# Closing four finished batches, and turning the next ones, one at a time inside the steps of a gated graph network

## The chip, the cores and the metric

The kernel runs on one core of one Trainium2 chip. The time is the device time of the whole program in microseconds (us), the median of several executions. The kernel before takes 1812.43 us (1811.12 to 1814.71 in 4 runs beside the changed kernel). All runs told of here, of both kernels and of every experiment, are in the fast state. The clock that TensorE was granted, as a mean over a run, lay between 0.995 and 0.999 of full speed, except in the three kernels in which TensorE stops longest: `closing_only` (0.990 to 0.992), `pin_turn` (0.985 to 0.988) and `pin_order34` (0.982 to 0.985). The experiments ran in three later calls on other chips; the kernel before took 1813.1, 1812.22 and 1812.23 us there, so differences of 1 us between experiments of different calls say nothing. The spans in the profiles are about 2 us shorter than the times, so spans are compared with spans and times with times.

## The reference, cut to what matters

```python
def _L1_gnn_ref(input, in_matrix, out_matrix, w3_w, ..., time_step):     # both matrices are adj
    def step(h, _):
        m_in  = jnp.einsum('nm,bmd->bnd', in_matrix, h)
        m_out = jnp.einsum('nm,bmd->bnd', out_matrix, h)
        av = jnp.concatenate([m_in, m_out], axis=-1)
        u3 = h @ u3_w.T + u3_b
        z = sigmoid(av @ w3_w.T + w3_b + u3)
        r = sigmoid(av @ w4_w.T + w4_b + u3)
        hv = tanh(av @ w5_w.T + w5_b + (r * h @ u5_w.T + u5_b))
        h = (1.0 - z) * h + z * hv
    ...                                                     # 5 steps

x = _layernorm(x + _L0_gnn_ref(x, adj, ...), axis=-1)       # x: 16 batches of 1024 x 128
x = _layernorm(x + _L1_gnn_ref(x, adj, adj, ...), axis=-1)
```

All is float32. The kernel takes the 16 batches in four groups of four. A group goes through its five steps, and then it has to be *closed*: the last h is added to the saved x, and the sum is normalized and stored.

## The kernel before: the parts that matter

h lies in two layouts. `rows` has nodes on the partitions, for the products with adj; `hid` has features on the partitions, for the gates. Within a step a batch goes from `hid` to `rows` by a VectorE turn of 32x32 blocks and a trip over DRAM (`turn_rows`, `fetch_rows`). At a change of group two more turns are needed: the last h goes back to node rows for the closing, and the first h of the next group, which was loaded as rows, goes to `hid`.

```python
    y_of = [ypad[0], ypad[1], hvs.rearrange("p h x -> p (h x)"), ypad[0]]

    def finish_early(q, k):                    # closing, first half: by TensorE
        nc.sync.dma_start(y_of[k], saved_rows(q * QUAD + k))
        finish(q, k, y_of[k])                  # two times: 4 transposes, then a VectorE add out of PSUM

    def turn_hidden(k, stage):                 # turn of the next first h: 4 small VectorE turns a batch
        ...
        for q in range(NQ): for s in range(STEPS):          # cut
            ...
                else:                          # first step of the next group
                    outer_sums(rows)
                    before = [call(finish_early, q - 1, k) for k in range(QUAD)]
                    norm = [call(normalize, q - 1, k, y_of[k]) for k in range(QUAD)]
                    fetch = [call(fetch_hidden, k) for k in range(QUAD)]
                    hooks = {
                        12: {5: [before[1]], 2: [fetch[0], before[2]], "end": [fetch[1], before[3]]},
                        3: {1: [fetch[2]], 2: [fetch[3]]},
                        67: {6: [norm[1]], 7: [norm[2]], 4: [norm[3]]},
                        54: {"end": [call(drain, 99, 0)]},
                    }
```

The products with adj come in four chains, `12`, `3`, `67` and `54`; each has seven products (1 to 7) that go through three banks of PSUM and are taken out by a copy or an add:

```python
        after = {
            1: lambda: nc.scalar.copy(fb, fa),
            ...
            7: lambda: nc.vector.tensor_add(x22, fb, x22),    # frees bank pb for product 4
            3: lambda: nc.vector.tensor_add(x12, fc, x12),
            4: lambda: nc.scalar.copy(x21, fb),               # the gates of the step need this one
        }
```

A hook `{67: {1: f}}` is run while the program is written, ahead of product 1 of chain `67`. What is not pinned is put into an engine's queue by the planner that lays the program out, so the order in a queue is partly the planner's.

Of the kernel before, what the change touches and what calls it, by code (L numbers as in the profile page):

```python
# [15 lines left out]
STEPS = 5  # L16
# [4 lines left out]
def kernel(  # L21
# [63 lines left out]
    turned = [dram.tile([16, P, 64], F32, name=f"turned{i}") for i in range(3)]  # L85
    hidden = [dram.tile([16, P, 64], F32, name=f"hidden{i}") for i in range(QUAD)]
# [146 lines left out]
    def layernorm(y, tag, store, now=False):  # L233
# [4 lines left out]
        for c in range(n + 1):  # L238
            if c < n:
                pin(nc.vector.bn_stats(stats[:, c, :], y[:, c, :]))  # L240
            if c > 0:
                pin(nc.vector.bn_aggr(mv[:, c - 1, :], stats[:, c - 1, :]))
# [16 lines left out]
        if now == "DVE":  # L259
            for c in range(n):  # L260
                nc.vector.tensor_scalar(
                    y[:, c, :], y[:, c, :], mv[:, c, 0:1], rstd[:, c : c + 1],
                    ALU.subtract, ALU.mult,
                )
            put()
        elif now:
            for c in range(n):
                apply(c)
            put()
        else:  # L270
            for c in range(n):
                waiting.append((slot[0], lambda c=c: tc.keep_in_program_order(apply(c))))
            waiting.append((slot[0], put))

# [48 lines left out]
    def chain(tag, src, turned, ns, results, hooks, order=(1, 5, 6, 2, 7, 3, 4)):  # L323
# [32 lines left out]
        for a in order:  # L356
# [12 lines left out]
            with tc.high_priority():  # L369
                after[a]()  # L370
# [145 lines left out]
    def turn_rows(k, h=None):  # L516
        cols, n = half_of(h)
        t = ypad[k % 2][:, cols]
        op = nc.vector.transpose(
            t.rearrange("p (to n j c) -> p n to c j", to=4, n=n, c=2),  # L520
            hid[:, k, cols].rearrange("p (n to i c) -> p n to c i", to=4, n=n, c=2),
        )
        tc.keep_in_program_order(nc.sync.dma_start(
            between(k, h).rearrange("g p x -> p g x"), t.rearrange("p (g x) -> p g x", x=64)
        ))
        return op

    def fetch_rows(k, h=None):
        cols, n = half_of(h)
        src = between(k, h).rearrange("(to n) (s j) x -> to j (n s) x", n=n, s=4)  # L530
        for to in range(4):
            tc.keep_in_program_order(nc.sync.dma_start(
                rows[ts(to, SQ), k, cols].rearrange("j (m x) -> j m x", x=64), src[to]
            ))

    def turn_hidden(k, stage):

        v = rows[:, k].rearrange("p (n c a j) -> p n c a j", n=4, c=2, a=4)
        for f in range(2):
            t = stage(f)  # L540
            for a in range(2):
                nc.vector.transpose(
                    t[:, ts(a, QT)].rearrange("p (n i c) -> p n c i", n=4, c=2),
                    v[:, :, :, 2 * f + a],
                )
            nc.sync.dma_start(
                hidden[k][ts(f, 8)].rearrange("g p x -> p g x"),
# [10 lines left out]
    def to_hidden(k):  # L558
        turn_hidden(k, lambda f: agg[:, 2 * (k % 2) + f, HALF:])
        fetch_hidden(k)  # L560
# [93 lines left out]
    y_of = [ypad[0], ypad[1], hvs.rearrange("p h x -> p (h x)"), ypad[0]]  # L654

    def finish_early(q, k):
        nc.sync.dma_start(y_of[k], saved_rows(q * QUAD + k))
        finish(q, k, y_of[k])
# [42 lines left out]
    for q in range(NQ):  # L701
        for s in range(STEPS):
            tag = f"{q}_{s}"
            if s == 0:
# [11 lines left out]
                else:  # L716
                    outer_sums(rows)
                    before = [call(finish_early, q - 1, k) for k in range(QUAD)]
                    norm = [call(normalize, q - 1, k, y_of[k]) for k in range(QUAD)]
                    fetch = [call(fetch_hidden, k) for k in range(QUAD)]  # L720
                    hooks = {
                        12: {5: [before[1]], 2: [fetch[0], before[2]], "end": [fetch[1], before[3]]},
                        3: {1: [fetch[2]], 2: [fetch[3]]},
                        67: {6: [norm[1]], 7: [norm[2]], 4: [norm[3]]},
                        54: {"end": [call(drain, 99, 0)]},
                    }
            else:
                hooks = {54: {}}
            hooks[54][4] = [call(gate_half, tag, 0, 0)]
            aggregate(tag, rows, hooks, s > 0)  # L730
            last = s == STEPS - 1
            end = last and q == NQ - 1
# [8 lines left out]
            gates(tag, 1)  # L741
            update(tag, 0, not last)
            if not last:
                fetch_rows(0)
            gates(tag, 2)
            update(tag, 1, not last)
            if last:
                finish_early(q, 0)
                normalize(q, 0, y_of[0])
                for k in range(2):  # L750
                    turn_hidden(k, lambda f: first[:, k, ts(f, HALF)])
            else:
                fetch_rows(1)
            gates(tag, 3)
            if last:
                sums_of(rows, (1, 2))
                sums_of(rows, (3,))
                for k in range(2):
                    turn_hidden(2 + k, lambda f: first[:, k, ts(f, HALF)])
            update(tag, 2, not last)  # L760
            update(tag, 3, not last)
# [35 lines left out]
```

## Time and profile before

| | kernel before |
|---|---|
| median time | 1812.43 us |
| span in the profile | 1810.0 us |
| one inner step | 77.17 us |
| the last step of a group with the first of the next | 159.29, 159.00, 160.43 us |
| data moved by DMA | 140.37 MB, 78 GB/s |

The prediction below shows the busy table, the three changes and an inner step. Two views that it leaves out matter later. The first is an inner step that is longer than the others, in the table by stage (stretch, length, then busy time of TensorE, weight loads, VectorE, ScalarE and GpSimd with instruction counts, granted clock, DMA share, GB/s):

```profile
778.22:856.52 78.30, 77.41 (x278) 53.23 (x276) 52.87 (x76) 31.45 (x52) 0.00 (x0) 1.00 0.26 58
```

TensorE is idle here for 0.89 us: VectorE had waited 1.41 us for a fetch of `rows` (781.02), and its sum of line 289 came late. Nothing in the prediction counts this wait, and it is one that another layout can lose by chance. The second is the end of chain `54` on TensorE in an inner step (start, duration, instruction):

```profile
1135.83 1.03 PE L361 MATMUL pc<-e,tsum 128*128 128x256 f32 x4
1136.85 1.14 PE L361 MATMUL pb<-s,inner 128*128 128x256 f32 x4
1137.82 1.03 PE L361 MATMUL pb<-a,inner 128*128 128x256 f32 x4
1138.68 1.03 PE L361 MATMUL pc<-e,tsum 128*128 128x256 f32 x4
```

Product 3 (into pc) is split: four matmuls, then product 4 (into pb), then the other four. Four matmuls should start 0.86 us before the next group, as the last two rows do. Here the distances are 1.02 and 0.97, so the split costs 0.27 us, and it does so in every inner step of this kernel.

### The profile page before, as it was taken

The page shows a single profiled execution, that of the slowest core. Times are in us where ns is not written, and L with a number is a line of the kernel's source. Part 1 is how long each engine was busy: PE and PEld are TensorE (multiplying, and loading weights), DVE is VectorE, ACT ScalarE, POOL GpSimd, SP SyncE. Part 2 cuts the span into 40 slices and gives each one's busy share as a digit, 9 for nine tenths or more (in the row PEclk, how much of TensorE's full clock was granted, in tenths as well). Part 3 has the DMA queues.
Part 4 walks back from the last instruction along what each step waited for, and adds up shares of the span by engine and source line. Part 5 has one row for each costly group of instructions (what it writes and reads, how often), then busy time and mean ns, then how long its engine had stood idle before and what let it go on. Part 6 is the DMA issues. An engine that isn't in the chain of part 4 may idle for free.

```text
span 1810.0 us, 19922 instructions
## 1 busy us (share of the span) xinstructions
PE 1787.7 (99%) x6805; PEld 1269.2 (70%) x6805; DVE 1293.8 (71%) x2316; ACT 793.4 (44%) x1418; POOL 98.0 (5%) x142
## 2 busy tenths in 40 slices
PE   8999999999999999999999999999999999999998
PEld 7888884866758576675857757586675858667584
DVE  7987776676766958576676957667577775767667
ACT  2345555344342554434244463434434553443426
POOL 0112220000000010000000200000000100000004
PEclk9999999999999999999999999999999999999999
DMA  6233262140323334132142423214043331403222
GB/s 224 71 128 138 95 158 68 32 93 12 82 47 93 91 97 93 23 71 51 43 106 81 93 70 70 62 32 93 12 105 95 92 83 23 93 18 76 52 54 82
DMA packets 352564, 140.37 MB, mean 78 GB/s; under 512 B 338128, under 2 KB 339024, under 8 KB 352464
## 3 DMA queue, kind: packets, MB, share of 16 engines
q1 hardware_dynamic: 351600, 135.96, 29.5%
q10 hardware_dynamic: 864, 3.15, 0.4%
q8 instruction: 54, 0.88, 0.2%
q14 instruction: 46, 0.38, 0.1%
HBM read 80.35 MB, written 58.72 MB: 77 GB/s over the span
## 4 chain that ended last, share of the span: by engine, by line
PE 87%; DVE 7%; DMA 2%; ACT 1%; POOL 1%; issue 1%; SPq 0%; DVEq 0%; POOLq 0%
PE pb L361 23%; PE pa L361 13%; PE pc L361 12%; PE pu L462 7%; PE pu L451 7%; PE seeded L467 7%; PE ph L480 7%; PE ph L479 7%; PE pc_x L361 2%; PE pa_x L361 2%; PE seeded L428 1%; DMA rows<-saved 1%; POOL rstd L246 1%; PE pt L566 1%; DVE agg L411 1%
## 5 line engine op out<-in xcount | busy, mean ns | idle before, releaser
L361 PE MATMUL pb<-e,inner 128*128 128x256 f32 x864 | 206.7, 380 | 3.7 <-ACT pb L347 2.6
L466 DVE TENSOR_TENSOR tsum<-tsum,hid 128x512 f32<-128x512 f32 x160 | 107.1, 683 | 114.6 <-ACT tsum L465 114.2
L361 PEld LDWEIGHTS pb<-e,inner 128*128 128x128 f32 x864 | 167.1, 194 | 24.6 <-ACT pb L347 4.2
L490 ACT ACTIVATE tsum<-ph,bh 128x512 f32<-128x512 f32 x158 | 108.6, 687 | 145.0 <-PE ph L480 144.8
L462 PE MATMUL pu<-agg,w_t 128*128 128x512 f32 x320 | 166.0, 608 | 0.5 <-DVE agg L411 0.5
L480 PE MATMUL ph<-tsum,u_t 128*128 128x512 f32 x320 | 163.5, 592 | 0.1
L496 DVE TENSOR_TENSOR tsum<-tsum,hid 128x512 f32<-128x512 f32 x158 | 108.1, 684 | 77.6 <-ACT tsum L490 77.4
L479 PE MATMUL ph<-agg,w_t 128*128 128x512 f32 x320 | 163.5, 592 | 0.0
L467 PE MATMUL seeded<-agg,w_t 128*128 128x512 f32 x320 | 161.0, 592 | 0.0
L451 PE MATMUL pu<-hid,u_t 128*128 128x512 f32 x320 | 152.0, 594 | 2.0 <-DVE ypad L574 2.0
L361 PE MATMUL pb<-s,inner 128*128 128x256 f32 x576 | 151.3, 385 | 0.3 <-DVE agg L351 0.2
L361 PE MATMUL pb<-a,inner 128*128 128x256 f32 x576 | 144.6, 379 | 0.0
L465 ACT ACTIVATE tsum<-pu,br 128x512 f32<-128x512 f32 x160 | 110.2, 688 | 74.3 <-PE pu L462 69.9
L361 PE MATMUL pc<-e,inner 128*128 128x256 f32 x560 | 134.3, 379 | 0.3 <-DVE inner L288 0.3
L361 PEld LDWEIGHTS pb<-s,inner 128*128 128x128 f32 x576 | 108.7, 194 | 24.8 <-DVE rows L351 10.7
L470 ACT ACTIVATE tsum<-seeded,bz 128x512 f32<-128x512 f32 x160 | 109.9, 687 | 27.2 <-PE seeded L467 23.6
L361 PEld LDWEIGHTS pb<-a,inner 128*128 128x128 f32 x576 | 111.5, 194 | 14.1 <-issue 1.9
L361 PEld LDWEIGHTS pc<-e,inner 128*128 128x128 f32 x560 | 108.8, 195 | 12.3 <-PE pa L361 0.6
L498 DVE TENSOR_TENSOR hid<-hid,tsum 128x512 f32<-128x512 f32 x158 | 109.0, 690 | 10.1 <-DVE tsum L497 0.5
L480 PEld LDWEIGHTS ph<-tsum,u_t 128*128 128x128 f32 x320 | 60.7, 190 | 77.0 <-issue 72.9
L467 PEld LDWEIGHTS seeded<-agg,w_t 128*128 128x128 f32 x320 | 60.8, 190 | 76.6 <-issue 76.6
L479 PEld LDWEIGHTS ph<-agg,w_t 128*128 128x128 f32 x320 | 60.5, 190 | 75.4 <-issue 72.7
(181 smaller groups left out, 2859.3 us busy)
## 6 DMA issues: line engine op xcount, KB each, us to landing
turned<-ypad SPq DMA_DIRECT2D x48, 512.0 KB, 3.8
rows<-turned SPq DMA_DIRECT2D x192, 128.0 KB, 2.8
rows<-saved SPq DMA_DIRECT2D x20, 512.0 KB, 3.4
hid<-hidden SPq DMA_DIRECT2D x64, 128.0 KB, 3.4
turned<-ypad SPq DMA_DIRECT2D x32, 256.0 KB, 2.9
rows<-turned SPq DMA_DIRECT2D x128, 64.0 KB, 2.1
hid<-in_x_dram SPq DMA_DIRECT2D x12, 512.0 KB, 4.2
hidden<-first SPq DMA_DIRECT2D x24, 256.0 KB, 3.0
```

The source lines that it names most:

```text
L361: product = nc.tensor.matmul(bank_of[a][:, ts(o, QT)], chunk(a, o, c), left[n][a][:, c, :], start=(a in (1, 5) and o == 0 and c == 0), sto ...
L451: pin(nc.tensor.matmul(pu, w_t["u3"], hid[:, k, ts(h, HALF)], start=True, stop=True, skip_group_check=True))
L462: pin(nc.tensor.matmul(pu, w_t["w4"], agg[:, k, cols], start=False, stop=True, skip_group_check=True))
L465: pin(nc.scalar.activation(rh[:, cols], pu, AF.Sigmoid, bias=br))
L466: pin(nc.vector.tensor_mul(rh[:, cols], rh[:, cols], hid[:, k, cols]))
L467: pin(nc.tensor.matmul(pz, w_t["w3"], agg[:, k, cols], start=False, stop=True, skip_group_check=True))
L470: pin(nc.scalar.activation(z[:, cols], pz, AF.Sigmoid, bias=bz))
L479: pin(nc.tensor.matmul(ph, w_t["w5"], agg[:, k, cols], start=True, stop=False))
L480: pin(nc.tensor.matmul(ph, w_t["u5"], rh_of[k % 2][:, cols], start=False, stop=True))
L490: pin(nc.scalar.activation(hv, ph, AF.Tanh, bias=bh))
L496: pinned(nc.vector.tensor_sub(hv, hv, hid[:, k, cols]))
L498: pinned(nc.vector.tensor_add(hid[:, k, cols], hid[:, k, cols], hv))
```

## The change

The closing leaves TensorE. In the last step of a group each batch is turned by VectorE in one 128x1024 instruction and stored to DRAM; in each of the next four steps one batch is fetched back, added, normalized and stored, in chain `54`. The turn of the next first h also goes into the steps, one batch in each, in chain `67`. The core of the diff:

```diff
+    closing = [dram.tile([16, P, 64], F32, name=f"closing{i}") for i in range(QUAD)]
...
-                pin(nc.vector.bn_aggr(mv[:, c - 1, :], stats[:, c - 1, :]))
+                last_stats[0] = pin(nc.vector.bn_aggr(mv[:, c - 1, :], stats[:, c - 1, :]))
...
-            with tc.high_priority():
+            behind = tc.issue_after(closed[0].ins) if closed[0] else nullcontext()
+            with tc.high_priority(), behind:
                 after[a]()
...
-    def finish_early(q, k):
-        nc.sync.dma_start(y_of[k], saved_rows(q * QUAD + k))
-        finish(q, k, y_of[k])
+    spare = hvs.rearrange("p h x -> p (h x)")
+
+    def close_load(q, k):
+        fetch_rows(k, None, closing[k], ypad[0])
+        tc.keep_in_program_order(nc.sync.dma_start(spare, saved_rows(q * QUAD + k)))
+
+    def close(q, k):
+        t = ypad[0].rearrange("p (n d c) -> p n c d", n=4, c=2)
+        y = spare.rearrange("p (n c d) -> p n c d", n=4, c=2)
+        tc.keep_in_program_order(nc.vector.tensor_add(y, y, t))
+        strict[0] = True
+        layernorm(chunked(spare), f"1_{q * QUAD + k}", as_rows(q * QUAD + k, out))
+        strict[0], closed[0] = False, last_stats[0]
+
+    def next_load(q, k):
+        tc.keep_in_program_order(nc.sync.dma_start(spare, saved_rows(q * QUAD + k)))
+
+    def next_turn(k):
+        turn_hidden(k, spare, [ypad[1]])
...
-                    before = [call(finish_early, q - 1, k) for k in range(QUAD)]
-                    norm = [call(normalize, q - 1, k, y_of[k]) for k in range(QUAD)]
-                    ...                                             # and their hooks
+            k = s if q else s - 1
+            if q < NQ - 1 and 0 <= k < QUAD:
+                hooks[3] = {1: [call(next_load, q + 1, k)]}
+                hooks[67] = {1: [call(next_turn, k)]}
+            if q > 0 and s > 0:
+                hooks.setdefault(67, {})[5] = [call(close_load, q - 1, s - 1)]
+                hooks[54] = {6: [call(close, q - 1, s - 1)]}
...
+                if last:
+                    turn_rows(k, None, closing[k])
+                    fetch_hidden(k)
```

Two things are easy to overlook. The one buffer `hvs` (`spare`) serves the turn and the closing of a step, one after the other. And `behind` puts every later add of `after` behind the last statistics of a closing in VectorE's queue.

More of the change, by code (lines that the diff above doesn't have):

```diff
@@ L273, in layernorm @@
             waiting.append((slot[0], put))
+    last_stats, closed = [None], [None]
     waiting = deque()
@@ L514, in between, with turn_rows @@
         return turned[k % 2] if h is None else turned[2][ts(h, 8)]
-    def turn_rows(k, h=None):
+    def turn_rows(k, h=None, to=None):
         cols, n = half_of(h)
+        to = between(k, h) if to is None else to
         t = ypad[k % 2][:, cols]
@@ L523, in turn_rows, with fetch_rows, turn_hidden @@
         tc.keep_in_program_order(nc.sync.dma_start(
-            between(k, h).rearrange("g p x -> p g x"), t.rearrange("p (g x) -> p g x", x=64)
+            to.rearrange("g p x -> p g x"), t.rearrange("p (g x) -> p g x", x=64)
         ))
         return op
-    def fetch_rows(k, h=None):
+    def fetch_rows(k, h=None, come=None, dst=None):
         cols, n = half_of(h)
-        src = between(k, h).rearrange("(to n) (s j) x -> to j (n s) x", n=n, s=4)
+        come = between(k, h) if come is None else come
+        dst = rows[:, k] if dst is None else dst
+        src = come.rearrange("(to n) (s j) x -> to j (n s) x", n=n, s=4)
         for to in range(4):
             tc.keep_in_program_order(nc.sync.dma_start(
-                rows[ts(to, SQ), k, cols].rearrange("j (m x) -> j m x", x=64), src[to]
+                dst[ts(to, SQ), cols].rearrange("j (m x) -> j m x", x=64), src[to]
             ))
-    def turn_hidden(k, stage):
-        v = rows[:, k].rearrange("p (n c a j) -> p n c a j", n=4, c=2, a=4)
-        for f in range(2):
-            t = stage(f)
-            for a in range(2):
-                nc.vector.transpose(
-                    t[:, ts(a, QT)].rearrange("p (n i c) -> p n c i", n=4, c=2),
-                    v[:, :, :, 2 * f + a],
-                )
+    def turn_hidden(k, y, stage):
+        v = y.rearrange("p (n c a j) -> p a n c j", n=4, c=2, a=4)
+        w = 4 // len(stage)
+        for f, t in enumerate(stage):
+            if w == 4:
+                nc.vector.transpose(t.rearrange("p (a n i c) -> p a n c i", a=4, n=4, c=2), v)
+            else:
+                for a in range(w):
+                    nc.vector.transpose(
+                        t[:, ts(a, QT)].rearrange("p (n i c) -> p n c i", n=4, c=2),
+                        v[:, w * f + a],
+                    )
             nc.sync.dma_start(
-                hidden[k][ts(f, 8)].rearrange("g p x -> p g x"),
+                hidden[k][ts(f, 4 * w)].rearrange("g p x -> p g x"),
                 t.rearrange("p (g x) -> p g x", x=64),
@@ L558, in to_hidden @@
     def to_hidden(k):
-        turn_hidden(k, lambda f: agg[:, 2 * (k % 2) + f, HALF:])
+        turn_hidden(k, rows[:, k], [agg[:, 2 * (k % 2) + f, HALF:] for f in range(2)])
         fetch_hidden(k)
@@ L651 @@
             aggregate(f"x{q}", room, hooks, False)
-    y_of = [ypad[0], ypad[1], hvs.rearrange("p h x -> p (h x)"), ypad[0]]
-    def finish_early(q, k):
-        nc.sync.dma_start(y_of[k], saved_rows(q * QUAD + k))
-        finish(q, k, y_of[k])
+    spare = hvs.rearrange("p h x -> p (h x)")
[13 more added lines that the diff above has]
+        turn_hidden(k, spare, [ypad[1]])
     def ending(q, tag):
@@ L717 @@
                     outer_sums(rows)
-                    before = [call(finish_early, q - 1, k) for k in range(QUAD)]
-                    norm = [call(normalize, q - 1, k, y_of[k]) for k in range(QUAD)]
-                    fetch = [call(fetch_hidden, k) for k in range(QUAD)]
-                    hooks = {
-                        12: {5: [before[1]], 2: [fetch[0], before[2]], "end": [fetch[1], before[3]]},
-                        3: {1: [fetch[2]], 2: [fetch[3]]},
-                        67: {6: [norm[1]], 7: [norm[2]], 4: [norm[3]]},
-                        54: {"end": [call(drain, 99, 0)]},
-                    }
+                    hooks = {54: {}}
             else:
                 hooks = {54: {}}
+            last = s == STEPS - 1
+            end = last and q == NQ - 1
+            k = s if q else s - 1
[5 more added lines that the diff above has]
+                hooks[54] = {6: [call(close, q - 1, s - 1)]}
             hooks[54][4] = [call(gate_half, tag, 0, 0)]
             aggregate(tag, rows, hooks, s > 0)
-            last = s == STEPS - 1
-            end = last and q == NQ - 1
             if end:
@@ L740 @@
                 break
-            gates(tag, 1)
-            update(tag, 0, not last)
-            if not last:
-                fetch_rows(0)
-            gates(tag, 2)
-            update(tag, 1, not last)
-            if last:
-                finish_early(q, 0)
-                normalize(q, 0, y_of[0])
-                for k in range(2):
-                    turn_hidden(k, lambda f: first[:, k, ts(f, HALF)])
-            else:
-                fetch_rows(1)
-            gates(tag, 3)
-            if last:
-                sums_of(rows, (1, 2))
-                sums_of(rows, (3,))
-                for k in range(2):
-                    turn_hidden(2 + k, lambda f: first[:, k, ts(f, HALF)])
-            update(tag, 2, not last)
-            update(tag, 3, not last)
+            for k in range(QUAD):
+                if k < QUAD - 1:
+                    gates(tag, k + 1)
+                if last and k == QUAD - 2:
+                    sums_of(rows, (1, 2))
+                    sums_of(rows, (3,))
+                update(tag, k, not last)
+                if last:
+                    turn_rows(k, None, closing[k])
+                    fetch_hidden(k)
+                elif k < QUAD - 2:
+                    fetch_rows(k)
             if not last:
```

## The prediction

> **What bounds the kernel now.** I read the page's busy table first, then the table by stage (windows), then the timelines of one inner step engine by engine.
>
> The busy table, columns engine, busy us, share, instructions:
>
> ```profile
> PE 1787.7 (99%) x6805; PEld 1269.2 (70%) x6805; DVE 1293.8 (71%) x2316; ACT 793.4 (44%) x1418; POOL 98.0 (5%) x142
> ```
>
> TensorE is busy in 99% of 1810.0 us. Such a number is only a hint, so I looked for a period. In the chain of waits, the product that opens a step (pu from line 451, six instructions) starts at 856.68, at 933.85, then at 1092.85, 1170.02 and 1247.18. One inner step is therefore 77.17 us, and two steps that hold a change of batch group take 159 us. The windows below are the three changes of group (last step of one group with first step of the next), then one inner step; columns: stretch, its length, then busy time of each engine with instruction counts.
>
> ```profile
> 541.93:701.22 159.29, 158.70 (x585) 109.01 (x585) 117.05 (x234) 75.07 (x136) 10.61 (x16) 1.00 0.36 93
> 933.85:1092.85 159.00, 158.69 (x585) 109.01 (x585) 117.20 (x234) 75.15 (x136) 10.61 (x16) 1.00 0.37 93
> 1324.35:1484.78 160.43, 158.94 (x585) 108.93 (x585) 116.90 (x233) 75.07 (x136) 10.61 (x16) 1.00 0.36 89
> 1092.85:1170.02 77.17, 77.17 (x278) 53.32 (x277) 52.85 (x76) 31.44 (x52) 0.00 (x0) 1.00 0.24 55
> ```
>
> An inner step has TensorE busy for its whole 77.17 us: no waits to win there. Two of them are 154.34 us, so the three changes of group cost 4.95, 4.66 and 6.09 us more: 15.70 us in all, less than 0.9% of the run. That is everything this change can touch, apart from what it may spoil.
>
> What those microseconds are, in the TensorE timeline around the second change:
>
> ```profile
> 1012.41 1.89 PE L361 MATMUL pa<-a,rows 128*128 128x256 f32 x8
> 1014.14 1.11 PE L566 MATMUL pt<-ident,hid 128*128 128x128 f32 x8
> 1015.09 1.89 PE L361 MATMUL pc<-e,inner 128*128 128x256 f32 x8
> ```
>
> The group of eight turns of one closed batch takes the place from 1014.14 to 1015.09, 0.95 us (start to start; 1.11 is with the pipelined end). Four groups are 3.8 us per change, 11.4 for three. The remaining 4.3 us are waits: TensorE waits of 2.0 us on the VectorE add behind those turns (line 574), and short breaks.
>
> **What the Trainium skill says.** "TensorE: Matmul & The Clock Gate", section "Part 4: PE-mode transpose", says that only TensorE turns a full 128x128, into PSUM so that a VectorE pass must follow, at about 275 ns in a kernel. The trace agrees on one (283 ns median) but eight in a row are paced at 0.12 us each, so the 12 groups are cheaper than 96 times 275 ns. "VectorE: DVE Perf Modes", section "The three transpose paths", says that VectorE turns only 32x32 blocks: hence the trip over DRAM to put the blocks in place. The trace has such a turn already (line 519, 128x1024, mean 1248 ns). The same page's section on the TRN2 errata gives (N+151)/0.96 ns for an f32 add; for 1024 that is 1224 ns, and the trace has 1216 to 1226. "DMA: Bandwidth & Descriptors", section "Issuing engines are not separate DMA queues", says that all transfers share the 16 engines; here they are a quarter to a third busy, and the new transfers come from the sync queue as the old.
>
> **The change part by part.**
>
> Removed at each change of group: 32 TensorE turns (4 times 0.95 us on the path); eight VectorE adds out of PSUM (0.68 us each, 5.1); 16 small VectorE turns of the next first h (0.42 each, 6.6); four normalizations; all bunched where VectorE has 117 us of work in 159. Only the first item is TensorE time; the others cost through the waits above.
>
> Added there: four VectorE turns 128x1024 of the last h, 1.25 us each, with their stores; they take the place of the turns an inner step makes anyway (three full and two halves), so the last step is for VectorE an inner step. The new h is fetched into hid per batch as soon as the old is turned; its first reader is at least 30 us on in the next step, against 3.4 us to landing. So I expect the pair at 154.5 to 155 us.
>
> Moved into inner steps, one batch in each:
> - Turn of the next first h: 12 times one 1.25 us turn on VectorE, in the chain of products 6 and 7. The VectorE timeline of the step starting 1092.85 has room there: idle 4.24 us before 1123.77.
> - Closing: 12 times one add of 128x1024 (1.22), eight bn_stats (0.265) and eight bn_aggr (0.166). Summed, 4.7 us; but the statistics overlap, as a run of them at the second change shows:
>
> ```profile
> 1004.93 0.16 DVE L242 BATCH_NORM_AGGREGATE mv<-stats 128x2 f32<-128x6 f32 x1
> 1005.02 0.25 DVE L240 BATCH_NORM_STATS2 stats<-ypad 128x6 f32<-128x128 f32 x1
> 1005.19 0.16 DVE L242 BATCH_NORM_AGGREGATE mv<-stats 128x2 f32<-128x6 f32 x1
> 1005.27 0.25 DVE L240 BATCH_NORM_STATS2 stats<-ypad 128x6 f32<-128x128 f32 x1
> ```
>
> A pair every 0.26 us: eight take 2.1, with the last 0.2, and 1.15 for the add at its pitch: an estimate of 3.5 us. They are put behind the add of line 404 and ahead of the add of line 351 in the last chain. The inner step has this hole:
>
> ```profile
> 1130.42 1.22 DVE L404 TENSOR_TENSOR agg<-agg,rows 128x1024 f32<-128x1024 f32 x1
> 1136.10 0.69 DVE L351 TENSOR_TENSOR rows<-pb,rows 128x512 f32<-128x512 f32 x1 [4.46 <-PE pb L361]
> ```
>
> Between 1131.64 and 1136.10 are 4.46 us in which VectorE waits for TensorE. 3.5 fit with about 1 us over. The data must be there by 1131.6: their load is hooked some 15 us before and transfers land in 2.8 to 3.8 us.
> - GpSimd then takes about 2.7 us (of it the power 1.67), to about 1138. Then ScalarE applies eight times at a pitch of 0.40, 3.2 us, just where this step has
>
> ```profile
> 1138.89 0.58 ACT L353 COPY rows<-pb 128x512 f32<-128x512 f32 x1 [4.00 <-PE pb L361]
> 1139.50 0.69 DVE L411 TENSOR_TENSOR agg<-rows 128x512 f32<-128x512 f32 x1 [2.71 <-ACT rows L353]
> 1140.61 0.69 ACT L465 ACTIVATE tsum<-pu,br 128x512 f32<-128x512 f32 x1 [1.14 <-PE pu L462]
> ```
>
> This is the narrow place. TensorE's next products wait for the add of line 411, that for the copy of line 353, and that now stands among eight applies. The before kernel shows what this costs: in the step after the second change, ScalarE had six applies there (1053.24, 2.41 us) and TensorE showed two breaks of 0.16 and 0.11 us. I take these 0.27 and round up to 0.35 us for each closing, because there GpSimd was long done and here it may be just late: 12 times, 4.2 us given back. It comes from one place, so it is the weakest number.
>
> Sum: -15.7 (all the excess), +0.9 (0.3 us of breaks left at each change, a choice), +4.2 (closings), +0.0 (turns in the 4.24 us hole) = -10.6 us. 1812.35 - 10.6 = 1801.75, say 1801.7 us.
>
> **The rivals.**
>
> (a) The closing does not fit its hole. Each microsecond over the hole in 12 steps is 12 us, so with 1 us over, the gain is gone (about 1812), and with 2 us over, the kernel is 12 us slower (1824). For it: the hole has only about 1 us to spare, and product 4 must wait until line 351 has read the bank pb, so a late end reaches TensorE at once. Against: when line 351 is late, TensorE has the rest of product 3 to do first (0.86 us), which it already splits for this.
>
> (b) ScalarE becomes the wait: applies placed in issue order ahead of the copies that free pu, while GpSimd is still at its power. Then the gate products stall up to 3 us per closing, 12 times 3 = 36 us: 1837. For it: the before kernel has five such ScalarE waits on GpSimd, and at the longest, 2.87 us before 86.95 in layer 0, a copy to pb stood behind the apply and TensorE stopped for 2.58 us. Against: that was one in five; the others were 0.36 to 0.76 us; here ScalarE has 4 us idle before line 353 that cover most of GpSimd's time, and the eight applies of line 251 in the ending (1784.20, 3.18 us) stand amid gates with no break of TensorE.
>
> (c) The transfers are late: one sync queue in order, with nine or so issues added per step. It would show as VectorE waiting on the closing or hidden transfers. Between 1107 and 1153 the queue issued nothing in this step, so I give it little; if the load were 5 us late in 12 steps it would cost tens of us.
>
> (d) The wait part of the gain does not come: only the 11.4 us of TensorE turns go and the 4.3 us of waits turn into others, such as sums on the newly loaded rows. With the closings as above that is 1812.35 - 11.4 + 4.2 = 1805.2.
>
> **Range and chances.** The best case is the whole 15.7 with nothing given back, 1796.6. Middle 1801.7; (d) gives 1805, and with closings twice as dear 1809; part of (a) or (b) gives 1811. So 8 in 10 in 1796.5 to 1811. Faster by over 2% means below 1776, and needs more than twice the whole excess: 0.01. Slower by over 2% means above 1848.6, so 36 us lost net, which is (b) and (a) together or a bad (c): 0.02. Within 2%: 0.97.
>
> **What will show it.** Right: no turns of TensorE but the 24 of the ending's first three batches; the pair of steps at a change 154.5 to 155 us; steps with a closing 77.3 to 77.7 us and steps without one 77.17; statistics ending before line 351's add and that add still waiting for TensorE. TensorE busy lower by about 11 to 13 us in the page. Wrong: steps with a closing above 78 us, with TensorE waiting on the add of line 351 (rival a), on ScalarE's copies (b), VectorE on a transfer (c), or a pair at a change still above 156 (d). A gain over 16 us would mean that inner steps held slack that I did not see.

## The result, and the profile after

The changed kernel takes 1799.16 us (1798.27 to 1800.58, 4 runs) against 1812.43 us. The ratio is 0.9926, with a 95% interval of 0.9909 to 0.9943, so it counts as the same within 2%. Ratios here and below are the mean time of one kernel's fast runs over that of the other's of the same rounds, so not quite the ratio of the medians quoted. The prediction was 1801.7, range 1796.5 to 1811: the time is inside the range and 2.5 us below the middle.

The busy row of the page:

```profile
PE 1775.3 (99%) x6709; PEld 1259.2 (70%) x6709; DVE 1309.0 (73%) x2280; ACT 789.3 (44%) x1418; POOL 94.5 (5%) x142
```

TensorE lost 12.4 us of work and 96 instructions: the 12 groups of eight turns. VectorE has 15.2 us more in 36 instructions fewer: at the changes 24 adds out of PSUM and 48 small turns went, and 36 turns and adds of about 1.2 us came. The steps, each from the opening product of the gates to the next step's:

| stretch | before, us | after, us | difference |
|---|---|---|---|
| start to the first such product | | | +0.71 |
| three steps of group 0 | 77.16, 77.33, 77.16 | 77.26, 77.30, 77.16 | +0.07 |
| three changes of group | 159.29, 159.01, 160.44 | 154.92, 155.06, 155.00 | -13.76 |
| eight steps of groups 1 to 3 | 77.17, 78.30, 77.16; 77.16, 77.17, 77.16; 77.16, 77.17 | 77.13, 76.91, 76.92; 77.55, 77.51, 76.92; 77.25, 77.24 | -1.02 |
| rest (ending) | 171.05 | 171.25 | +0.20 |
| sum | | | -13.8 |

The sum is the difference of the spans, 1810.0 - 1796.2. In the same view by stage as before, the first change, two kinds of step and the second change:

```profile
542.54:697.46 154.92, 154.70 (x553) 105.29 (x552) 106.68 (x152) 62.86 (x104) 0.00 (x0) 1.00 0.34 82
774.59:851.50 76.91, 76.91 (x277) 53.50 (x276) 57.34 (x94) 34.14 (x60) 2.36 (x4) 1.00 0.37 89
928.42:1083.48 155.06, 154.78 (x553) 105.24 (x552) 108.70 (x168) 65.26 (x112) 2.36 (x4) 1.00 0.35 85
1083.48:1161.03 77.55, 77.38 (x278) 53.26 (x276) 57.30 (x94) 34.13 (x60) 2.35 (x4) 1.00 0.37 89
```

Where GpSimd has four instructions, a batch was closed. Of the 12 closings eight lie in the eight steps, two in the second and third change, and two in the ending. A step with a turn and a closing has 4.5 us more VectorE work than the inner step of before (57.3 against 52.85; with a closing alone, in the last group, 56.17), and in the second row TensorE is busy for all its 76.91 us. One closing, in order of time (in brackets: idle time before, and who ended it):

```profile
736.54 1.22 DVE L677 TENSOR_TENSOR hvs<-hvs,ypad 128x1024 f32<-128x1024 f32 x1
...
739.75 0.30 DVE L243 BATCH_NORM_AGGREGATE mv<-stats 128x2 f32<-128x6 f32 x2
...
740.53 1.67 POOL L247 TENSOR_TENSOR rstd<-rstd,power 128x8 f32<-128x8 f32 x1
...
741.08 0.69 DVE L354 TENSOR_TENSOR rows<-pb,rows 128x512 f32<-128x512 f32 x1 [1.03 <-PE pb L364]
...
742.85 1.27 ACT L252 ACTIVATE hvs<-hvs,shift,rstd 128x128 f32<-128x128 f32 x3 [2.97 <-POOL shift L249]
...
744.47 0.58 ACT L356 COPY rows<-pb 128x512 f32<-128x512 f32 x1 [0.36 <-PE pb L364]
```

The add starts at 736.54, the statistics end at 740.05: 3.5 us. The add out of bank pb (line 354) then still waits 1.03 us for TensorE. ScalarE stands 2.97 us at the first apply, waiting for GpSimd; three applies are done when the copy of line 356 comes, at 744.47, and this copy still waits 0.36 us for TensorE. So it is not late, but only by 0.36 us.

The turn of the next h stands elsewhere than I had put it. In a 77.5 us step:

```profile
1104.42 1.24 DVE L550 STREAM_TRANSPOSE ypad<-hvs 128x1024 f32<-128x1024 f32 x1
1105.59 1.18 DVE L324 TENSOR_TENSOR tsum<-rows,tsum 128x1024 f32<-128x1024 f32 x1
1106.69 0.41 DVE L354 TENSOR_TENSOR agg<-pb,agg 128x256 f32<-128x256 f32 x1
```

The planner put it among back-to-back sums, so the bank add behind it (1106.69) is 1.2 us later. In the two 77.5 us steps TensorE stops for this add:

```profile
1107.16 1.14 PE L364 MATMUL pb<-s,inner 128*128 128x256 f32 x4 [0.17 <-DVE agg L354]
```

From start to start this costs 0.34 us, and 0.16 and 0.08 more in the two groups behind it: nearly all of the 0.6 us between the 76.92 and the 77.5 us steps. The turn stands in this place in all six steps of groups 1 and 2. In the 77.13 us step it costs TensorE 0.21 us (0.13 and 0.08, at 720.75 and 721.74), in the three steps of 76.91 and 76.92 us nothing. These three in turn are 0.25 us *shorter* than any inner step before, because product 3 of chain `54` is no longer split. That holds for all six steps; in the last group it is still split, and the steps take 77.25 and 77.24 us.

### The profile page after: what moved, and what is told of

Read it like the earlier page. It is cut to its first block, busy times and chain, and to the rows that moved or that the text cites. A ratio compares the mean times of both kernels' runs of the same rounds, so it can differ in the third digit from the quotient of the medians.

```text
span 1796.2 us, 19819 instructions
## 1 busy us (share of the span) xinstructions
PE 1775.3 (99%) x6709; PEld 1259.2 (70%) x6709; DVE 1309.0 (73%) x2280; ACT 789.3 (44%) x1418; POOL 94.5 (5%) x142
## 2 busy tenths in 40 slices
DMA packets 404212, 159.23 MB, mean 89 GB/s; under 512 B 388241, under 2 KB 389137, under 8 KB 404113
## 4 chain that ended last, share of the span: by engine, by line
PE 89%; DVE 6%; issue 1%; DMA 1%; POOL 1%; ACT 1%; SPq 0%; DVEq 0%; POOLq 0%
PE pb L364 22%; PE pc L364 12%; PE pa L364 12%; PE pu L467 8%; PE pu L456 8%; PE seeded L472 7%; PE ph L485 7%; PE ph L484 7%; PE pc_x L364 2%; PE pa_x L364 2%; PE seeded L433 1%; POOL rstd L247 1%; DVE tsum L324 1%; DMA rows<-in_x_dram 1%; ACT ypad L252 1%
## 5 line engine op out<-in xcount | busy, mean ns | idle before, releaser
L485 PEld LDWEIGHTS ph<-tsum,u_t 128*128 128x128 f32 x320 | 60.8, 190 | 76.9 <-issue 72.1
```

Source lines behind the costliest of these rows:

```text
L485: pin(nc.tensor.matmul(ph, w_t["u5"], rh_of[k % 2][:, cols], start=False, stop=True))
```

## The experiments

Twelve kernels ran, each in five rounds beside the kernel before. Eleven gave the right result; one is wrong by a mistake of mine and is told as such.

**Moving the turns alone.** Does the turn of the next first h earn anything by itself? The kernel before, with `next_load` and `next_turn` in the steps and no turns of the next h at the change; the closing stays with TensorE.

```diff
+            if q < NQ - 1 and s > 0:
+                hooks[3] = {1: [call(next_load, q + 1, s - 1)]}
+                hooks[67] = {1: [call(next_turn, s - 1)]}
...
-                for k in range(2):
-                    turn_hidden(k, lambda f: first[:, k, ts(f, HALF)])      # twice, at the change
```

> The kernel before, with only the turns of the next first h moved into the steps (one per step, s = 1 to 4); closing stays at the change of group, with its 32 TensorE turns. Theory (TensorE's own turns are most of the gain, 3.8 us per change): the pair of steps at a change takes 158 to 159 us and the whole 1808 to 1811 us, hardly faster than before. Rival (VectorE's crowd at the change, of which the 16 small turns are a large part, is what cost): the pair falls below 156.5 us and the whole to 1804 us or less.

Measured: 1812.33 us, ratio 0.9996 (0.9988 to 1.0004). The changes of group take 158.79, 159.18 and 160.41 us, as before. This part alone gains nothing, much as theory had it (the time is even above its 1808 to 1811 us), and the rival is out. That the 32 turns on TensorE and the adds behind them set the length of the change fits this; it is the next test that takes them away.

**Closing alone.** The changed kernel, with the turns of the next h back at the change, staged in the tile `first`.

```diff
-            if q < NQ - 1 and 0 <= k < QUAD:
-                hooks[3] = {1: [call(next_load, q + 1, k)]}
-                hooks[67] = {1: [call(next_turn, k)]}
...
+                if last and k in (2, 3):
+                    j = 2 * (k - 2)
+                    for i in range(2):
+                        turn_hidden(j + i, rows[:, j + i], [first[:, i, ts(f, HALF)] for f in range(2)])
```

> The changed kernel, with the turns of the next first h back at the change of group (16 small VectorE turns there), closing still spread. Theory: the pair of steps at a change takes 155 to 155.5 us and inner steps with a closing 76.9 us (no turn in VectorE's crowded stretch), the whole 1798 to 1800 us, as the changed kernel. Rival (the crowd at the change costs): the pair above 156.5 us, the whole 1804 us or more.

Measured: 1832.18 us, ratio 1.0104 (1.009 to 1.0118), and a wrong result (relative error 0.149): my edit fetched two batches of h ahead of their turn. The time says nothing about the question, but the waits say what staging at the change risks. From the list of waits (total, times, longest) and, under it, the same list for the stretch from 570 to 640 us:

```profile
PE pa L364 <- ACT first L353: 23.0, 3, 7.7
```

```profile
ACT first L353 <- DMA hidden<-first: 7.2, 1, 7.2
```

TensorE stopped three times for 7.7 us, because a copy into `first` had to wait until the store of the staged turn had left it, and that store stood behind others in the queue. The mended version turns batches 2 and 3 ahead of the third update and fetches each h only after its turn.

```diff
+                    for i in range(2):
+                        turn_hidden(2 + i, rows[:, 2 + i], [first[:, i, ts(f, HALF)] for f in range(2)])
                 update(tag, k, not last)
                 if last:
+                    if k == 1: ...                  # the same for batches 0 and 1
                     turn_rows(k, None, closing[k])
-                    fetch_hidden(k)
+                    if k > 0:
+                        fetch_hidden(k - 1)         # and the last one behind k == 3
```

> As closing_only, mended: the turns of the next first h are traced ahead of the fetches that read them (the first try read old data and was wrong), and their stores stand ahead of the last two closing stores in the queue, so that the staging tile is free for the next step. Theory: the pair of steps at a change takes 155 to 156.5 us, a step with a closing 77.2 us, the whole 1799 to 1803 us. Rival (the crowd of turns and transfers at the change keeps TensorE waiting whatever the order): the pair above 158 us, the whole 1808 us or more.

Measured: 1802.98 us, ratio 0.9953 (0.9939 to 0.9966), right result. The changes take 156.38, 156.94 and 156.42 us, 9.0 us less than before in all, where both parts together save 13.8. Steps with a closing take 77.24 or 77.25. TensorE still waits at the changes:

```profile
PE pa L364 <- ACT first L353: 3.7, 3, 1.2
```

The theory is met but for one change, 0.44 us above its 156.5. So the closing carries two thirds of the gain at the changes, and the turns, worth nothing alone, are worth the other 4.8 us once the closing has left: 3.7 of them are these waits. Some of these come from my order of the stores, so the split is not exact.

**Without the order behind the statistics.**

```diff
-            behind = tc.issue_after(closed[0].ins) if closed[0] else nullcontext()
-            with tc.high_priority(), behind:
+            with tc.high_priority():
                 after[a]()
```

> The changed kernel without the order that puts later bank adds behind the last statistics of a closing. Theory (that order makes TensorE do product 3 whole ahead of product 4, which saves 0.25 us per closing): product 3 is split in two again with a break of 0.16 us, steps with a closing take 0.2 to 0.4 us longer than in the changed kernel, the whole 1801 to 1803 us. Rival (the order does nothing for the time): 1798.5 to 1800.5 us as before.

Measured: 1811.63 us, ratio 0.9991 (0.9983 to 1.0): nearly the whole gain is gone, far more than either theory gave it. Six closings cost 2.1 us each: the six steps of groups 1 and 2 take 79.13, 79.75, 79.13, 79.20 and, the last two together, 158.25 us, 12.5 us more than in the changed kernel. The closings in the changes (155.01 and 155.00 us) and in the last group (77.24), where the planner put the add of line 354 behind the statistics without help, cost nothing. The order of one of the dear ones:

```profile
738.76 0.26 DVE L241 BATCH_NORM_STATS2 stats<-hvs 128x6 f32<-128x128 f32 x1
...
740.53 0.69 DVE L354 TENSOR_TENSOR rows<-pb,rows 128x512 f32<-128x512 f32 x1 [1.50 <-PE pb L364]
...
741.40 0.30 DVE L243 BATCH_NORM_AGGREGATE mv<-stats 128x2 f32<-128x6 f32 x2
...
744.50 1.26 ACT L252 ACTIVATE hvs<-hvs,shift,rstd 128x128 f32<-128x128 f32 x3 [5.18 <-POOL shift L249]
...
745.66 0.56 ACT L356 COPY rows<-pb 128x512 f32<-128x512 f32 x1
...
747.01 1.13 PE L466 MATMUL pu<-agg,w_t 128*128 128x512 f32 x2 [1.42 <-DVE agg L415]
```

The add out of the bank stands among the statistics and waits 1.50 us for TensorE; the statistics behind it wait with it and end at 741.70 instead of 740.05 (though this step began 0.35 us earlier). GpSimd starts 1.65 us later, ScalarE's applies too, and the copy of line 356, queued behind three of them, comes at 745.66 instead of 744.47. TensorE then stops for 1.42 us at the gates. The Trainium skill, "PSUM — Partial Sum Buffer", section "Engine vs sequencer instructions", says that the queues of ScalarE, VectorE and GpSimd are strictly first in, first out. The trace agrees: one waiting add of VectorE passes through three queues and comes out as a stop of TensorE.

**Is GpSimd on the path?** One way to ask: the power is done twice in each closing (its first result is overwritten), 1.67 us more of GpSimd, with TensorE's order left as it was.

```diff
+        if closing_now[0]:
+            nc.gpsimd.tensor_tensor(shift, rstd, power[:, :n], ALU.pow)
         nc.gpsimd.tensor_tensor(rstd, rstd, power[:, :n], ALU.pow)
```

> The changed kernel with GpSimd's power done twice in each of the twelve closings (1.67 us later); TensorE's order of instructions is identical. Theory (ScalarE waits 2.97 us for GpSimd in each closing and TensorE does not notice, but only 0.36 us of ScalarE's idle time are left before line 356's copy): the copy is 1.3 us late, TensorE waits about 1 us per closing, the whole is 8 to 16 us slower than the changed kernel, 1807 to 1815 us. Rival (b was never near): within 2 us of the changed kernel.

Measured: 1818.83 us, ratio 1.0036 (1.0023 to 1.0049): 19.7 us more than the changed kernel, 1.64 us for each of 12 closings, that is nearly all of the 1.67 us added.

```profile
745.20 1.26 ACT L254 ACTIVATE hvs<-hvs,shift,rstd 128x128 f32<-128x128 f32 x3 [5.03 <-POOL shift L251]
...
746.37 0.56 ACT L358 COPY rows<-pb 128x512 f32<-128x512 f32 x1
```

```profile
PE pu L469 <- DVE agg L418: 17.6, 12, 2.4
```

TensorE stops in all 12 closings, 17.6 us in total. So rival (b) of the prediction was not far off: the path from the statistics over GpSimd to the copy is as good as full. The loss is above the 8 to 16 us that I had expected.

The counter-test: the same, but the applies, and the store of the closed batch with them, are released one product later, so that the applies stand behind the copy in ScalarE's queue.

```diff
-                waiting.append((slot[0], lambda c=c: tc.keep_in_program_order(apply(c))))
+                waiting.append((slot[0] + late, lambda c=c: tc.keep_in_program_order(apply(c))))
-            waiting.append((slot[0], put))
+            waiting.append((slot[0] + late, put))
```

> As pow_x2 (GpSimd 1.67 us later in each closing), but the applies are issued one product later, behind the copy of product 4's bank. TensorE's order is the same. Theory (the late applies hurt only because they stand ahead of that copy in ScalarE's queue): the 20 us are back, 1797 to 1802 us. Rival (GpSimd's lateness hurts in another way): 1810 us or more.

Measured: 1802.15 us, ratio 0.9948 (0.9936 to 0.9961). With the same doubled power 16.7 us are back.

```profile
745.28 0.56 POOL L252 TENSOR_SCALAR shift<-shift 128x8 f32<-128x8 f32 x1
745.43 0.59 ACT L359 COPY rows<-pb 128x512 f32<-128x512 f32 x1 [4.59 <-PE pb L367]
745.92 2.42 ACT L255 ACTIVATE hvs<-hvs,shift,rstd 128x128 f32<-128x128 f32 x6
```

The copy goes first, at TensorE's call, and GpSimd can be late. So nearly all of what hurt was the place of the applies in ScalarE's queue. The 3 us that are missing belong mostly to the late release itself, as the next run shows: with the power once it takes only 0.85 us less.

Then is the changed kernel better with only this (`late`, and the power once)?

> The changed kernel with the applies of a closing one product later, behind the copy of product 4's bank; TensorE's order is the same. Theory: ScalarE's twelve waits of 2.97 us for GpSimd go, but TensorE did not feel them, so the whole is 1796.5 to 1800 us, the same as the changed kernel or a hair less. Rival (the copy did come late and cost the 0.35 us per closing of the prediction): 1794 to 1796 us.

Measured: 1801.3 us, ratio 0.9942 (0.9929 to 0.9954), if anything 2 us worse than the changed kernel, and both theory and rival missed. Two steps take 78.45 and 78.33 us, and TensorE waits three times for a VectorE sum (line 292, 1.8 us in total) that it had not waited for. The sum itself had waited each time, 1.46 to 2.20 us, for a fetch of `rows`. The trace shows why that may be: the store of the closed batch, which stood at 747.00 in a quiet queue, now comes at 780.41, among the stores and fetches of the next step. The edit moved two things, and this run does not part them.

**Is VectorE's hole full?** The statistics of each closing done twice, 2.1 us more, which is 1 us over the hole: the case of rival (a).

```diff
-        for c in range(n + 1):
+        for r in range(2 if closing_now[0] else 1):
+          for c in range(n + 1):
```

> The changed kernel with the statistics of each closing done twice (2.1 us more on VectorE, 5.6 us in a hole of 4.5). Theory: the add of line 354 is 1 us late, but TensorE has product 3 whole (1.73 us) and, as the planner orders it here, gate products to do first: 0 to 0.4 us per closing, 1799 to 1804 us. Rival (a of the prediction: every us over the hole is a us of TensorE): about 1.2 us per closing, 1811 us or more.

Measured: 1813.6 us, ratio 1.0005 (0.9997 to 1.0013): 14.4 us more than the changed kernel, near what rival (a) gives for an overrun of 1 us. But it is no clean test. The planner laid TensorE's order out anew (in part, product 4 behind gate products), and the span up to the first step is 3 us longer, in layer 0, where the edit changed nothing. The loss is also not spread as rival (a) says. In the six steps of groups 1 and 2, where that other order stands, the overrun costs 1.45 us in all, 0.24 us per closing, within the 0 to 0.4 us that I had expected. In the two changes and the two steps of the last group it costs 1.6 to 1.7 us each, and there TensorE stops for 1.46 or 1.47 us. So the agreement with rival (a) is partly chance. What is safe: where TensorE has no other work to put in between, the hole does not take 2.1 us more.

**The turn into the idle hole, as the prediction had it.** It is pinned behind the sums of its chain.

```diff
-                nc.vector.transpose(t.rearrange("p (a n i c) -> p a n c i", a=4, n=4, c=2), v)
+                tc.keep_in_program_order(
+                    nc.vector.transpose(t.rearrange("p (a n i c) -> p a n c i", a=4, n=4, c=2), v)
+                )
```

> The changed kernel with the turn of the next first h kept behind the sums traced before it, so that it falls in VectorE's hole of 3 to 4 us and not in its crowded stretch. Theory (the turn there delays the adds out of PSUM by 1.2 us and costs up to 0.6 us in some steps): no break of TensorE at the opening of the chain of products 6 and 7, the two steps of 77.5 us fall to 76.9, the whole to 1796.5 to 1798.5 us. Rival (TensorE's order of gate products, which the planner changes with it, matters more): 1799 us or more.

Measured: 1855.46 us, ratio 1.0234 (1.022 to 1.0248): slower by over 2%, a plain miss. The turn does stand in the hole (723.72), but the steps with both a turn and a closing take 86.5 to 87 us.

```profile
729.19 0.43 SPq L674 DMA_DIRECT2D hvs<-saved  x1
...
743.60 0.69 DVE L471 TENSOR_TENSOR tsum<-tsum,hid 128x512 f32<-128x512 f32 x1 [7.70 <-ACT tsum L470]
744.21 1.22 DVE L679 TENSOR_TENSOR hvs<-hvs,ypad 128x1024 f32<-128x1024 f32 x1
...
755.38 2.08 PE L467 MATMUL pu<-agg,w_t 128*128 128x512 f32 x2 [4.49 <-DVE agg L416]
```

The store of the turn holds the fetches behind it in the queue, so the closing's load of `hvs` is issued at 729.19 instead of 723.47. By the median landing time of this transfer, 4.1 us, it is there at 733.3, in time for a closing at 736. But the planner had put the closing's add *behind* the gate's product of line 471, which waits for ScalarE until 743.60. The data was not late; the queue was ordered as if it were.

Waits are not all of the loss. In this step TensorE waits 2.62 and 4.49 us, but the step is 9.8 us too long. After the second stop the granted clock (third number from the end) is half for a while:

```profile
755.00:760.00 5.00, 4.62 (x6) 2.04 (x7) 2.22 (x4) 2.99 (x7) 0.00 (x0) 0.50 0.26 105
```

Three pairs of products in a row, from 755.38 to 760.64, take 1.7 to 1.9 us from start to start instead of 0.86, which is 2.7 us more. In `closing_only` the first products behind the stop of 7.66 us show the same (at 638.89 four take 2.07 us, not 1.03). So in this kernel a long stop of TensorE costs more than its own length.

If the order of the queue is the cause, the pinned turn must be harmless once the four fetches of the closing are issued ahead of it:

```diff
+    def close_rows(k):
         fetch_rows(k, None, closing[k], ypad[0])
+
+    def close_load(q, k):
         tc.keep_in_program_order(nc.sync.dma_start(spare, saved_rows(q * QUAD + k)))
...
+                hooks.setdefault(3, {}).setdefault(1, []).append(call(close_rows, s - 1))
```

> As pin_turn, but the four fetches of the closed rows are issued in the chain of product 3, before the turn; only the load of the saved rows, which shares the turn's tile, still follows the turn. Theory (pin_turn lost 56 us because the late turn held up five transfers behind it in the queue, so that the planner put the closing's add behind a product that comes 8 us later): the add is back behind line 409 with its data there, TensorE's waits of 3 and 4.5 us are gone, the whole is 1797 to 1806 us (up to 0.9 us per closing where the planner puts product 4 first). Rival (the turn in the hole is itself what the step can't bear): 1840 us or more.

Measured: 1799.21 us, ratio 0.9925 (0.9912 to 0.9937).

```profile
724.78 1.25 DVE L551 STREAM_TRANSPOSE ypad<-hvs 128x1024 f32<-128x1024 f32 x1
...
736.78 1.22 DVE L681 TENSOR_TENSOR hvs<-hvs,ypad 128x1024 f32<-128x1024 f32 x1
```

56 us are back with the turn still in the hole, and the steps with a closing take 77.24 to 77.25, with the turn in them or, in the last group, without. The explanation holds. The kernel is no better than the changed kernel: the 77.5 us steps are gone, but so are the 76.9 us ones.

**Product 3 before product 4 everywhere.** If an unsplit product 3 saves 0.25 us in some steps, it might do so in all.

```diff
-            order=(1, 5, 6, 2, 7, 4, 3),
+            order=(1, 5, 6, 2, 7, 3, 4),
```

> The changed kernel with product 3 ahead of product 4 in the last chain of every aggregation, not only where a closing made it so. Theory (the split of product 3 costs 0.25 us per step): the steps without a closing fall from 77.16 to 76.9 us, the whole by 1.5 to 3 us, to 1796 to 1798 us. Rival (what follows product 4 is delayed instead, since its copy feeds the gates): no gain or a loss, 1799 us or more.

Measured: 1802.05 us, ratio 0.9949 (0.9935 to 0.9963). The theory fell. Steps without a closing gain 0.12 us (two of three), but those with one take 77.5 to 78.0:

```profile
PE pu L467 <- DVE agg L416: 6.2, 12, 2.1
```

The trace shows why, and it is not TensorE's order, which is the changed kernel's own in the first step with a closing (product 3 whole, then product 4). The edit also moved the applies: six of them, not three, now stand ahead of the copy of line 356 in ScalarE's queue (740.67, 2.42 us). The copy comes at 742.99, 0.7 us after product 4 would have let it start, and TensorE waits 0.37 us in each closing: rival (b) again. So what an unsplit product 3 is worth with the applies left in place was not measured. Both edits together:

> Both: the turn behind the sums and product 3 ahead of product 4. Theory: both gains add, 1794.5 to 1797 us, faster than both kernels. Rival: they touch the same waits or the planner's order spoils one of them, 1798 us or more.

Measured: 1862.73 us, ratio 1.0277 (1.0263 to 1.0291). It fails as the pinned turn does; the gains that the theory added up do not exist.

No version beat the changed kernel; the one with the turn pinned and the fetches early equals it.

## Why the prediction was right, point by point

- **What bounds the kernel.** Right. Reading the period of the steps, and not the 99% of TensorE, gave a ceiling of 15.7 us; 13.8 came. The Trainium skill, "Perfetto Trace Analysis", section "Identifying the Most-Contended Engine", says that the share of time in which matmuls are busy is no good measure of how close a kernel is to its limit; the trace agrees so far, that the same 99% stand in the page before and after. "No waits to win" in an inner step was read from one step: the step of 78.30 us had 0.89 us of them.
- **The change of group.** Predicted 154.5 to 155 us, measured 154.92, 155.06 and 155.00. The term "0.3 us of breaks left at each change" was too small: 0.58 to 0.72 are left over 154.34, so 13.7 us were saved and not 14.8. Most of it is one new wait: at 630.88, 1016.90 and 1403.89 TensorE waits 0.22 to 0.28 us for an add of line 354, which stands in VectorE's queue behind the last turn and the first sums of the new group. With the group behind it this costs 0.49, 0.55 and 0.51 us from start to start. TensorE's busy time fell by 12.4 us, in the predicted 11 to 13. Of rival (d) only this was seen: the waits on the add of line 574 (2.0 us) are gone, and 0.7 us of waits took their place.
- **The closings, "the weakest number".** Predicted 0.35 us each, 4.2 in all. Measured: the eight steps with a closing take 77.18 us on average against 77.17 for an undisturbed step before. This average hides three sizes: +0.08 where only a closing came in (two steps of the last group), -0.25 where product 3 became whole (six steps), and on top of that 0.21, 0.6 and 0.6 in the three of these six where the turn delayed a bank add. So this is the term that was mis-sized: the net cost is about 0, not 4.2. The 0.27 us that it was taken from were misread: breaks of 0.16 and 0.11 us stand at the switch to product 4 in every inner step of the kernel before, at 1135.83 above too, where no apply is near. The hole and the path, however, were read rightly: the add at 736.54, 3.5 us to the last statistics, 1 us over; "just late" for GpSimd is 0.36 us of room at the copy.
- **The turns, "+0.0 (turns in the 4.24 us hole)".** Wrong in its reason. The hole was empty, but the turn was not in it; the planner put it 6 us earlier, among sums. It cost two steps 0.6 us and one 0.2. Forcing it into the hole was ruinous until the fetches moved too; then the term did hold, for steps with the turn took no longer than steps without.
- **What the sum left out.** The wait of 0.89 us in one step of before went away with the new layout, and this longer step, 78.30 us against 77.17, gave back 1.1 us, which is luck; the start took 0.7 us more and the ending 0.2. With 13.8 at the changes these make the 13.8 of the spans. That the total came within 2.5 us owes something to errors that go opposite ways: the changes saved 1.1 us less than predicted and the start and the ending took 0.9 us more, while the closings cost about 4 us less and the lost wait gave 1.1.
- **Rivals.** (a) did not happen, because the statistics fit with 1.03 us over; an overrun of 1 us was costly when forced, except where TensorE had gate products to do first. (b) did not happen, by 0.36 us of room: forced, it cost 1.64 us per closing, and behind the copy under 0.1. The prediction had argued against it from ScalarE's 4 idle us, which was right, and took no account of how little was left of them. (c) TensorE never waited for a transfer of the closing, and among the waits of VectorE none on the new transfers stands; the trace puts five waits of ScalarE, of at most 0.9 us, down to them. All this although DMA moved 159.23 MB instead of 140.37.

What the prediction did not see at all: the gain hangs on one scheduling line. Without the order behind the statistics the same work takes 1811.63 us.

## What to carry to other kernels

When TensorE is full in every step, look for the stretches whose period is longer; their excess is the ceiling of the change, and work that leaves them for idle room in other steps can come close to free. Whether it does is decided by the order of each queue, not by the sum of busy time: here 1.67 us of GpSimd work ahead of the copy that TensorE waits for cost 1.64 us, and the same work cost next to nothing once the instructions of ScalarE that wait for it stood behind that copy. So after such a move, look at the idle time before the first few instructions behind the moved work, for that is the room that is left, and when an edit of one queue goes badly, look at what it did to the order of the others.

## What the Trainium skill lacked or had wrong

- "TensorE: Matmul & The Clock Gate" ("Part 4: PE-mode transpose") has about 275 ns for one transpose, and the trace agrees for one (283 ns); it lacks the rate of several in a row. Here eight take 0.95 us from start to start, 0.12 us each, so the time of one overstates 12 groups of eight by more than a factor of two.
- "PSUM — Partial Sum Buffer" says that the queues are first in, first out, but no page that I read says what follows for a moved piece of work: one waiting VectorE add in the wrong place cost 2.1 us in each of six closings, and 1.67 us of added GpSimd time came out as 1.64 us of TensorE time, or as 0.07 us when the applies stood behind the copy.
- No page gives a time for the batch-norm statistics instructions. On 128x128 f32 one takes 0.26 us, its aggregate 0.16 to 0.17 us, and interleaved a pair takes 0.26 us.
- "GPSIMD Engine Reference" has no figure for the power operation: on 128x8 f32 it takes 1.67 us (median), against 0.20 to 0.25 us for the multiplications and adds of the same size around it.
